# A graph network of two layers on one core: head outputs turned in 32x32 blocks by VectorE, and new aims for the planned order

## The chip, the cores and the metric

The kernel runs on one core of a Trainium2 chip. The core has TensorE (PE, matrix products into PSUM), VectorE (DVE), ScalarE (ACT), GpSimd (POOL) and SyncE (SP, which here only issues transfers), each with an instruction queue of its own. The metric is the device time in microseconds of one execution, the median of several runs.

## The reference, cut to what matters

There are 16 independent batches of N = 1024 nodes with 256 features. Layer 0 is attention with 8 heads of width 32; layer 1 is two graph attentions and a feed-forward part.

```python
# layer 0, for one batch
e = einsum('hqd,hkd->hqk', q, k)                 # q, k, v: 8 heads of 32 columns
e = where(e >= 0, e, 0.2 * e)
attn = softmax(where(adj > 0, e, NEG), axis=-1)
h = einsum('hqk,hkd->hqd', attn, v)              # head outputs
h = h.transpose to (n, 8 * 32)
out = layernorm(h, g1, b1)
out = concatenate([out, x], -1) @ Wffn.T
x1 = layernorm(out, g2, b2) + x
# layer 1: h = gat(gat(x1)); r = layernorm(x1 + h); layernorm(r + relu(r @ w_ff1) @ w_ff2)
```

The edit concerns the line of the head outputs and the division by the softmax's sums; the rest of the computation stays as it is.

## The kernel before, in words

All of a batch is computed with keys on the partitions. For head h and a tile t of 128 keys, `all_scores` (from L591) makes a score tile of 128 keys x 1024 queries in PSUM with two matmuls (L612). `weights` turns it into the tile `p`: ScalarE scales it by 0.2 (L628), VectorE takes the maximum with the scores (L630), ScalarE takes the exponential (L633), GpSimd multiplies by the mask of 0 and -1 (L637). Six `p` tiles exist at a time.

`all_values` multiplies the `p` tiles with V. One "product" is four matmuls side by side in four groups of 32 columns of the array: group i takes 256 queries of `p` and leaves 32 rows (the head's width) x 256 columns in partitions 32i to 32i+31 of `acc`, a PSUM bank. In the profile each of the four is recorded twice, as two passes over its 256 columns (L652). The left half of `acc` takes the product with V (stored negated), the right half the product with a tile of -1, which gives every partition of a group the same softmax sums. Two key tiles are taken at a time. For the first two pairs of a head VectorE first adds the two `p` tiles (L682, `add_pair`), so that six sums a head are made in place of eight.

`after_head` finishes a head. VectorE or ScalarE, whichever the planner finds free first, copies `acc` into an SBUF tile `ho` (L325 or L327 in `copy`); TensorE transposes `ho` in four 128x128 pieces into a PSUM bank `misc` (L702); VectorE takes the reciprocal of the sums (L707) and multiplies the outputs into `hn`, nodes on the partitions (L709). There are 128 heads in all. When a batch's eight heads are done, `rest` runs the remainder of the batch (transposes L369, products L778 and L781, the two graph attentions L863 to L926, feed-forward L966 and L994), beside the heads of the next batch.

The order on all five queues is fixed when the program is built. A planner (`Order`) keeps a clock for each engine, runs every part of the work as a thread whose steps state a cost (`yield on(PE=437)`), and puts next the ready step with the smallest "aim", a due time. Threads hold slots of counted buffers (three `misc` banks, one `acc`, six `p`, 18 `pair` tiles and others). The aims come from two tables, `EARLY` for the first two batches and `AIM` for the others, in units of a batch's slot of 253 us: `qk0` and `qk1` for the two halves of the next batch's Q and K projections, `v0` and `v1` for V, `graph0` and `graph1` for the graph attentions, `ff` for the feed-forward parts, `lead` for how early scores may start. `SWITCH` is the planner's cost of changing the shape in which TensorE is used ("single" for scores, "narrow" for products, None for the rest).

Transfers go out on two queues: x and the adjacency on ScalarE's, the projections' scratch writes, the stacks of Q and K that every head loads, x1 and the outputs on SyncE's.

Of the kernel before, what the change touches and what calls it, by code (L numbers as in the profile page):

```python
# [15 lines left out]
OP = mybir.AluOpType  # L16
# [18 lines left out]
class Order:  # L35
# [8 lines left out]
    SWITCH = {(None, "narrow"): 93.0, ("single", "narrow"): 93.0, ("narrow", None): 93.0,  # L44
              ("narrow", "single"): 197.0, (None, "single"): 84.0}
# [92 lines left out]
    def run(self):  # L138
        while self.active:
# [38 lines left out]
            if delay:  # L178
                self.transfers = max(self.transfers, end + 1000) + 1450 * max(1, round(cost / 500))
                th["ready"] = max(end + delay, self.transfers + 1200)  # L180
                th["last"] = None, 0
# [13 lines left out]
def wait(event):  # L195
    return "wait", event
# [37 lines left out]
def unshifted_path(  # L234
# [21 lines left out]
    ADDED = 2  # L256
# [144 lines left out]
    def mask_part(b, t, halves):  # L401
# [32 lines left out]
        yield on(PE=112 * n)  # L434
# [23 lines left out]
    def x_pair(b, u):  # L458
# [7 lines left out]
        yield on(PE=437)  # L466
# [47 lines left out]
    def v_part(b, g, u):  # L514
# [3 lines left out]
        yield on(PE=880)  # L518
# [72 lines left out]
    def all_scores():  # L591
        for b in range(B):
# [4 lines left out]
            for h in range(H):  # L597
                yield wait(("stack", b, h))
                q, kk = stacks[b, h]
                for t in range(NT):  # L600
# [8 lines left out]
                    yield on(PE=464, mode="single")  # L609
# [30 lines left out]
    def all_values():  # L640
        for b in range(B):
            for h in range(H):
# [7 lines left out]
                def product(w, p, at, first, last):  # L650
                    for i in range(4):
                        nc.tensor.matmul(acc[i * DH:(i + 1) * DH, at:at + QN], w, p[:, i * QN:(i + 1) * QN],  # L652
                                         start=first, stop=last)

                added = []
                for d in range(0, NT, GV):
                    last, adds = d + GV == NT, d < ADDED * GV
                    for t in range(d, d + GV):
                        yield wait(("p", b, h, t))
                    if added:  # L660
                        yield wait(("p added", b, h, d - GV))
                    yield aim(begin[b] + (h * NT + d + 2) / 2 * pace(b), SLOT)
                    ps = [probs.pop((b, h, t)) for t in range(d, d + GV)]
                    for t, p in zip(range(d, d + GV), ps):
                        yield on(PE=430, mode="narrow")
                        product(v[:, t, c:c + DH], p, 0, t == 0, False)
                        yield aim(begin[b], BIG)
                    if adds:
                        yield start(add_pair(b, h, d, ps), begin[b] + (h * NT + d + 2) / 2 * pace(b))
                    for p in added if adds else added + ps:  # L670
                        yield on(PE=430, mode="narrow")
                        product(minus_ones, p, QN, False, last and p is ps[-1])
                        yield give("p")
                    added = ps[:1] if adds else []
# [5 lines left out]
    def add_pair(b, h, d, ps):  # L680
        yield on(DVE=1180, shared=True)
        nc.vector.tensor_tensor(ps[0], ps[0], ps[1], op=OP.add)  # L682
        yield give("p")
        yield fire(("p added", b, h, d))

    def after_head(b, h, acc):
# [8 lines left out]
        engine = yield evacuate(HALF)  # L695
        copy(engine, ho, acc)
        yield give("acc")
        yield take("misc")
        pt = misc()
        yield on(PE=437)  # L700
        for i in range(TPH):
            nc.tensor.transpose(pt[:, i * P:(i + 1) * P], ho[:, i * P:(i + 1) * P], ident)  # L702
# [4 lines left out]
        nc.vector.reciprocal(rd, src[:, 1, :, :, 0])  # L707
        yield on(DVE=342)
        nc.vector.tensor_tensor(hn[b].rearrange("p (c i) d -> p i c d", i=2)[:, :, :, h * DH:(h + 1) * DH],  # L709
                                src[:, 0], rd[:, :, :, None].to_broadcast([P, 2, 4, DH]), op=OP.mult)  # L710
        yield give("misc")
# [39 lines left out]
    def rows_pair(b, u):  # L751
# [12 lines left out]
        yield on(PE=437)  # L764
# [26 lines left out]
        yield on(PE=437)  # L791
# [12 lines left out]
        for t in tiles:  # L804
            yield take("misc")
            pa = misc()
            yield on(PE=880)
# [28 lines left out]
    def first_half(b, s, nh):  # L836
# [7 lines left out]
        yield on(PE=437)  # L844
# [70 lines left out]
    def normed_pair(b, u, big, y2):  # L915
# [6 lines left out]
        for i, t in enumerate(tiles):  # L922
# [5 lines left out]
            yield on(PE=218)  # L928
# [10 lines left out]
        yield on(PE=437)  # L939
# [40 lines left out]
    def feed_forward(b, u, rT):  # L980
# [9 lines left out]
        for i in range(2):  # L990
# [5 lines left out]
            yield on(PE=218)  # L996
# [474 lines left out]
```

## Time and profile before

| | us |
|---|---|
| median of 3 runs (4397.36 to 4398.8) | 4397.64 |
| the profiled execution | 4397.53 |
| its span, first to last instruction | 4395.7 |
| TensorE matmuls busy | 4246.0 |
| VectorE busy | 3543.5 |
| ScalarE busy | 2979.7 |
| GpSimd busy | 2418.1 |

The span is that of the profiled execution; the 1.8 us beyond it lie before its first and after its last instruction. Busy time counts a matmul until its modelled end, so that overlapping matmuls count once. A line of the group list names the source line, the engine, the operation and its tiles, then the busy time in us and the mean ns of one instruction, and last the idle time just before these instructions with what ended it.

### The profile page before, as it was taken

Reading aid. Unit: us, or ns where it says so; the run is one execution under the profiler, and the core shown is the slowest. Engines: PE = TensorE matmul, PEld = TensorE weight load, DVE = VectorE, ACT = ScalarE, POOL = GpSimd, SP = SyncE. Lnnn points to the kernel's source line nnn. Section 1 sums busy time; section 2 is a strip of 40 time slices with the busy share of each in tenths; the row PEclk is TensorE's granted clock in tenths of the full one; section 3 lists DMA queues with packets and bytes.
Section 4 is the critical chain, followed back from the end, with each engine's and each line's share of the span. In section 5 each row is a group of like instructions: output and inputs, shape, how many; then the busy total and the mean of one; then the engine's idle time right before and its main releaser. Section 6 shows DMA issues by size and latency. Waiting matters only on the chain.

```text
span 4395.7 us, 77297 instructions
## 1 busy us (share of the span) xinstructions
PE 4246.0 (97%) x30539; PEld 3077.3 (70%) x30539; DVE 3543.5 (81%) x5525; ACT 2979.7 (68%) x4456; POOL 2418.1 (55%) x1033
## 2 busy tenths in 40 slices
PE   7888999999999999999999999999999999999898
PEld 4455767767677776767767677776767767677687
DVE  6878878878787888889788787888878788887853
ACT  6756667766767767776676767767776676766632
POOL 5856555554656646565564755636565564755700
PEclk9999999999999999999999999999999999999999
DMA  6423223232232323222232232313222232221100
GB/s 186 122 68 87 71 70 85 65 100 68 85 84 73 94 61 92 80 85 77 66 101 70 85 82 68 101 61 89 82 82 80 66 101 70 83 74 49 34 20 21
DMA packets 156287, 344.87 MB, mean 78 GB/s; under 512 B 21750, under 2 KB 24332, under 8 KB 155916
## 3 DMA queue, kind: packets, MB, share of 16 engines
q1 hardware_dynamic: 112140, 260.13, 20.5%
q10 hardware_dynamic: 43776, 79.71, 6.5%
q8 instruction: 243, 3.98, 0.4%
q14 instruction: 128, 1.05, 0.1%
HBM read 239.09 MB, written 100.66 MB: 77 GB/s over the span
## 4 chain that ended last, share of the span: by engine, by line
PE 81%; DVE 14%; ACT 3%; issue 2%; POOL 0%; DMA 0%; ACTq 0%; SPq 0%; DVEq 0%; POOLq 0%
PE ps_a L652 16%; PE ps_m L901 10%; PE ps_s L612 9%; PE ps_m L926 9%; PE ps_m L994 8%; PE ps_m L966 8%; DVE p L630 4%; PE ps_m L489 4%; PE ps_m L810 3%; DVE att L863 3%; PE ps_m L778 3%; PE ps_m L781 2%; DVE att L866 2%; PE ps_m L369 2%; PE ps_m L521 2%
## 5 line engine op out<-in xcount | busy, mean ns | idle before, releaser
L637 POOL TENSOR_TENSOR p<-p,mask 128x1024 f32<-128x1024 f32 x1024 | 2417.3, 2377 | 1752.1 <-ACT p L633 1401.4
L630 DVE TENSOR_TENSOR p<-p,ps_s 128x1024 f32<-128x1024 f32 x1024 | 1221.2, 1215 | 356.0 <-ACT p L628 351.5
L633 ACT ACTIVATE p<-p 128x1024 f32<-128x1024 f32 x1024 | 1080.2, 1060 | 343.3 <-DVE p L630 319.0
L628 ACT ACTIVATE p<-ps_s 128x1024 f32<-128x1024 f32 x1008 | 989.9, 1022 | 285.8 <-PE ps_s L612 202.5
L612 PE MATMUL ps_s<-qs,ks 128*128 128x512 f32 x2048 | 639.1, 430 | 35.5 <-DVE p L630 35.3
L652 PE MATMUL ps_a<-p,v 128*32 128x256 f32 x8192 | 564.1, 388 | 13.2 <-POOL p L637 12.6
L612 PEld LDWEIGHTS ps_s<-qs,ks 128*128 128x128 f32 x2048 | 350.0, 190 | 213.5 <-issue 68.0
L926 PE MATMUL ps_m<-y,att 128*128 128x256 f32 x2048 | 487.0, 382 | 5.8 <-ACT y L871 5.8
L901 PE MATMUL ps_m<-y,att 128*128 128x258 f32 x2048 | 482.8, 383 | 3.1 <-ACT y L871 2.6
L966 PE MATMUL ps_m<-rT,wf 128*128 128x256 f32 x2048 | 472.7, 381 | 13.2 <-ACT z L327 7.3
L994 PE MATMUL ps_m<-wf,hid 128*128 128x256 f32 x2048 | 475.3, 380 | 7.4 <-DVE hn L709 7.2
L901 PEld LDWEIGHTS ps_m<-y,att 128*128 128x128 f32 x2048 | 385.2, 190 | 85.6 <-issue 12.9
L966 PEld LDWEIGHTS ps_m<-rT,wf 128*128 128x128 f32 x2048 | 380.6, 190 | 81.8 <-issue 11.0
L652 PE MATMUL ps_a<-p,minus_ones 128*32 128x256 f32 x6144 | 408.7, 384 | 25.2 <-DVE p L682 25.2
L994 PEld LDWEIGHTS ps_m<-wf,hid 128*128 128x128 f32 x2048 | 379.9, 190 | 72.9 <-PE ps_a L652 12.2
L926 PEld LDWEIGHTS ps_m<-y,att 128*128 128x128 f32 x2048 | 376.7, 190 | 64.6 <-issue 8.6
L652 PEld LDWEIGHTS ps_a<-p,v 128*32 128x32 f32 x8192 | 209.0, 109 | 286.3 <-issue 143.3
L682 DVE TENSOR_TENSOR p<-p 128x1024 f32<-128x1024 f32 x256 | 385.4, 1506 | 25.7 <-PE ps_a L652 25.6
L863 DVE SCALAR_TENSOR_TENSOR att<-first,second 128x1024 f32<-128x1024 f32 x256 | 393.7, 1538 | 4.5 <-ACT first L850 4.5
L866 DVE SCALAR_TENSOR_TENSOR att<-mask,att 128x1024 f32<-128x1024 fp8e4 x256 | 353.0, 1379 | 5.9
L652 PEld LDWEIGHTS ps_a<-p,minus_ones 128*32 128x32 f32 x6144 | 198.7, 111 | 166.9 <-DVE p L682 32.1
L871 ACT ACTIVATE y<-y,check 128x258 f32<-128x258 f32 x256 | 130.8, 511 | 254.7 <-DVE check L869 254.2
(105 smaller groups left out, 4373.3 us busy)
## 6 DMA issues: line engine op xcount, KB each, us to landing
qs<-qk_halves SPq DMA_DIRECT2D x256, 256.0 KB, 4.1
ks<-qk_halves SPq DMA_DIRECT2D x256, 256.0 KB, 5.1
adj_i<-in_adj_dram ACTq DMA_DIRECT2D x240, 256.0 KB, 3.1
qk_halves<-high SPq DMA_DIRECT2D x128, 256.0 KB, 3.6
qk_halves<-low SPq DMA_DIRECT2D x128, 256.0 KB, 2.7
xr<-in_x_dram ACTq DMA_DIRECT2D x64, 256.0 KB, 2.7
x_kept<-x SPq DMA_DIRECT2D x64, 256.0 KB, 2.0
x<-x_kept SPq DMA_DIRECT2D x64, 256.0 KB, 3.4
```

The source lines that it names most:

```text
L612: nc.tensor.matmul(ps[:, cols], kk[:, t * P:(t + 1) * P], q[:, cols], start=True, stop=True)
L628: nc.scalar.activation(p, ps, AF.Copy, scale=ALPHA)
L630: nc.vector.tensor_tensor(p, p, ps, op=OP.max)
L633: nc.scalar.activation(p, p, AF.Exp)
L637: nc.gpsimd.tensor_tensor(p, p, mask_of(b, t), op=OP.mult)
L652: nc.tensor.matmul(acc[i * DH:(i + 1) * DH, at:at + QN], w, p[:, i * QN:(i + 1) * QN], start=first, stop=last)
L863: nc.vector.scalar_tensor_tensor(e, first[:, 0, :], second[:, j:j + 1], first[:, 1, :], op0=OP.mult, op1=OP.max)
L866: nc.vector.scalar_tensor_tensor(e, mask_of(b, j), -1.0, e, op0=OP.mult, op1=OP.mult, accum_out=sums[:, j:j + 1])
L901: nc.tensor.matmul(pa[:, cols:cols + width], big[:, j, i * P:(i + 1) * P], rows[:, j, :width], start=(j == 0), stop=(j == NT - 1))
L926: nc.tensor.matmul(pa[:, i * D:(i + 1) * D], big[:, j, t * P:(t + 1) * P], y2[:, j, :D], start=(j == 0), stop=False)
L966: nc.tensor.matmul(pa[:, i * 2 * P:(i + 1) * 2 * P], wf1[:, dc, hc * P:(hc + 1) * P], rT[:, dc, :], start=(dc == 0), stop=(dc == DC - 1))
L994: nc.tensor.matmul(pa[:, i * D:(i + 1) * D], hid[hc // 2][:, hc % 2, i * P:(i + 1) * P], wf2[:, hc, :], start=(hc == 0), stop=False)
```

## The change

Four things change.

The product takes its queries in another order: column group i takes, of each tile of 128 queries, the 32 with numbers 32i to 32i+31. The moving operand is then eight runs of 32 elements, 128 elements apart, and the output columns are ordered by tile and then by query in the run.

The head output is no longer copied and transposed by TensorE. VectorE's block transpose turns each 32x32 block of `acc` in place of the copy, PSUM to SBUF, and with the new order of queries the nodes then stand on the partitions as `hn` needs them. The reciprocal and the multiply read `ho` in SBUF.

The adding of `p` tiles is driven by tables (`JOINS`, `SUMMED`), which list the same two additions and six sums a head as before; a way of adding by a GpSimd transfer is written but not listed.

All values of `AIM` and `EARLY` are new, and so are `SWITCH` and several of the planner's costs, which touch the order of the instructions and nothing else.

```diff
-    SWITCH = {(None, "narrow"): 93.0, ("single", "narrow"): 93.0, ("narrow", None): 93.0,
-              ("narrow", "single"): 197.0, (None, "single"): 84.0}
+    SWITCH = {(None, "narrow"): 45.0, ("narrow", None): 250.0, ("narrow", "single"): 240.0}
...
-    ADDED = 2
+    JOINS = (('dve', 0, 1), ('dve', 2, 3))
+    SUMMED = ((0, 4), (2, 6), (4, 6), (5, 6), (6, 8), (7, 8))
+    JOINCOST = 950
+    JOINDELAY = 3600
...
-    AIM = dict(mask0=0.7454, x=0.7836, x_step=0.0012, mask=0.7416, mask_step=0.0241, qk0=0.8169, qk1=0.7629,
-               qk_step=0.0234, v0=0.8897, v1=0.9566, v_step=0.0513, rows=-0.1328, rows_step=0.039, first0=0.1101,
-               first1=0.2264, graph0=-0.041, graph1=0.3629, graph_step=0.0128, second=0.3518, second_step=0.0609,
-               normed=0.8572, normed_step=0.058, ff_wait=(None, 0, 1, 0), ff=(0.6792, -0.0021, 0.5781, 0.4984),
-               ff_step=0.0549, fast0=0.4291, fast1=0.9756, fast15=0.6646, lead=1.5024)
+    AIM = dict(mask0=0.5516, x=1.3927, x_step=-0.0171, mask=0.9041, mask_step=0.0013, qk0=0.7122, qk1=2.623,
+               qk_step=0.0074, v0=0.8646, v1=0.2387, v_step=-0.0163, rows=-0.0352, rows_step=0.0016, first0=0.4294,
+               first1=-0.1321, graph0=-0.0631, graph1=0.3632, graph_step=0.0462, second=0.6113, second_step=0.0151,
+               normed=1.0294, normed_step=0.0117, ff_wait=(None, 0, 1, 0), ff=(0.8041, 0.204, 3.2793, 1.5053),
+               ff_step=-0.1175, fast0=-0.0586, fast1=0.753, fast15=1.0361, lead=6.4585)
...
-    EARLY = dict(x=0.9697, x_step=0.0004, mask=0.7306, mask_step=0.0331, qk0=0.7893, qk1=0.9441, qk_step=0.026,
-                 v0=0.8496, v1=0.9733, v_step=0.0532, rows=-0.1833, rows_step=-0.0236, first0=0.1365,
-                 first1=-0.0311, graph0=-0.0903, graph1=-0.027, graph_step=0, second=0.3474, second_step=0.0327,
-                 normed=0.781, normed_step=0.02, ff_wait=(None, 0, 1, 0), ff=(0.6698, 0.0209, 0.488, 0.4266),
-                 ff_step=0.0422)
+    EARLY = dict(x=2.6793, x_step=-0.0501, mask=0.507, mask_step=0.0764, qk0=0.7919, qk1=0.9003, qk_step=-0.1061,
+                 v0=0.6048, v1=1.7324, v_step=-0.1383, rows=-2.2292, rows_step=-0.217, first0=-0.2174,
+                 first1=-4.0958, graph0=-0.094, graph1=-1.7727, graph_step=-0.0927, second=0.2445,
+                 second_step=0.079, normed=0.7931, normed_step=0.086, ff_wait=(None, 0, 1, 0),
+                 ff=(2.1852, 0.6139, 2.2145, 0.5745), ff_step=0.0569)
...
-        yield on(PE=437)
+        yield on(PE=460)
...
-        yield on(PE=880)
+        yield on(PE=895)
...
-                    yield on(PE=464, mode="single")
+                    yield on(PE=466, mode="single")
...
                 def product(w, p, at, first, last):
                     for i in range(4):
-                        nc.tensor.matmul(acc[i * DH:(i + 1) * DH, at:at + QN], w, p[:, i * QN:(i + 1) * QN],
+                        nc.tensor.matmul(acc[i * DH:(i + 1) * DH, at:at + QN].rearrange("d (t r) -> d t r", r=DH), w,
+                                         p.rearrange("k (t i r) -> k i t r", i=4, r=DH)[:, i],
                                          start=first, stop=last)
...
-                        yield on(PE=430, mode="narrow")
+                        yield on(PE=434, mode="narrow")
...
-    def add_pair(b, h, d, ps):
-        yield on(DVE=1180, shared=True)
-        nc.vector.tensor_tensor(ps[0], ps[0], ps[1], op=OP.add)
+    def join(b, h, n, ps):
+        how, to, by = JOINS[n]
+        for m in range(n):
+            if JOINS[m][1] in (to, by):
+                yield wait(("joined", b, h, m))
+        if how == "dve":
+            yield on(DVE=1180, shared=True)
+            nc.vector.tensor_tensor(ps[to], ps[to], ps[by], op=OP.add)
+        else:
+            yield on(POOL=JOINCOST, delay=JOINDELAY)
+            nc.gpsimd.dma_start(ps[to], ps[by], accum_op=OP.add)
         yield give("p")
-        yield fire(("p added", b, h, d))
+        yield fire(("joined", b, h, n))
...
         ho = buf([P, HALF], "pair", "ho")
-        engine = yield evacuate(HALF)
-        copy(engine, ho, acc)
+        yield on(DVE=600)
+        nc.vector.transpose(ho, acc)
         yield give("acc")
-        yield take("misc")
-        pt = misc()
-        yield on(PE=437)
-        for i in range(TPH):
-            nc.tensor.transpose(pt[:, i * P:(i + 1) * P], ho[:, i * P:(i + 1) * P], ident)
+        src = ho.rearrange("p (s t d) -> p s t d", s=2, d=DH)
+        rd = checks[b][:, h * NT:(h + 1) * NT]
+        yield on(DVE=205)
+        nc.vector.reciprocal(rd, src[:, 1, :, 0])
+        yield on(DVE=340, shared=True)
+        nc.vector.tensor_tensor(hn[b][:, :, h * DH:(h + 1) * DH], src[:, 0],
+                                rd[:, :, None].to_broadcast([P, NT, DH]), op=OP.mult)
         yield give("pair")
-        src = pt.rearrange("p (s i c d) -> p s i c d", s=2, i=2, d=DH)
-        rd = checks[b][:, h * NT:(h + 1) * NT].rearrange("p (c i) -> p i c", i=2)
-        yield on(DVE=235)
-        nc.vector.reciprocal(rd, src[:, 1, :, :, 0])
-        yield on(DVE=342)
-        nc.vector.tensor_tensor(hn[b].rearrange("p (c i) d -> p i c d", i=2)[:, :, :, h * DH:(h + 1) * DH],
-                                src[:, 0], rd[:, :, :, None].to_broadcast([P, 2, 4, DH]), op=OP.mult)
-        yield give("misc")
```

More of the change, by code (lines that the diff above doesn't have):

```diff
@@ L178, in run @@
             if delay:
-                self.transfers = max(self.transfers, end + 1000) + 1450 * max(1, round(cost / 500))
+                self.transfers = max(self.transfers, end + 1000) + (2700 if engine == "POOL" else
+                                                                    1450 * max(1, round(cost / 500)))
                 th["ready"] = max(end + delay, self.transfers + 1200)
@@ L433, in mask_part @@
         pairs = ab.bitcast(BF)
-        yield on(PE=112 * n)
+        yield on(PE=30 + 140 * n)
         for i in range(2 * n):
@@ L651, in product @@
                     for i in range(4):
-                        nc.tensor.matmul(acc[i * DH:(i + 1) * DH, at:at + QN], w, p[:, i * QN:(i + 1) * QN],
+                        nc.tensor.matmul(acc[i * DH:(i + 1) * DH, at:at + QN].rearrange("d (t r) -> d t r", r=DH), w,
+                                         p.rearrange("k (t i r) -> k i t r", i=4, r=DH)[:, i],
                                          start=first, stop=last)
-                added = []
+                ps = {}
+                begun = 0
@@ L656, in all_values @@
                 for d in range(0, NT, GV):
-                    last, adds = d + GV == NT, d < ADDED * GV
+                    last = d + GV == NT
                     for t in range(d, d + GV):
                         yield wait(("p", b, h, t))
[L660 to L664, printed above, removed]
-                        yield on(PE=430, mode="narrow")
-                        product(v[:, t, c:c + DH], p, 0, t == 0, False)
-                        yield aim(begin[b], BIG)
@@ L668, in all_values @@
[L668 to L672, printed above, removed]
+                    now = [t for t, at in SUMMED if at == d + GV]
+                    for t in now:
+                        for n in range(begun):
+                            if JOINS[n][1] == t:
+                                yield wait(("joined", b, h, n))
@@ new lines, in all_values @@
+                    due = begin[b] + (h * NT + d + 2) / 2 * pace(b)
+                    yield aim(due, SLOT)
+                    for t in range(d, d + GV):
+                        ps[t] = probs.pop((b, h, t))
+                        yield on(PE=434, mode="narrow")
+                        product(v[:, t, c:c + DH], ps[t], 0, t == 0, False)
+                        yield aim(begin[b], BIG)
+                    while begun < len(JOINS) and max(JOINS[begun][1:]) < d + GV:
+                        yield start(join(b, h, begun, ps), due)
+                        begun += 1
@@ L673, in all_values @@
+                    for t in now:
+                        for n in range(begun):
+                            if JOINS[n][1] == t:
+                                yield wait(("joined", b, h, n))
+                        yield on(PE=434, mode="narrow")
+                        product(minus_ones, ps[t], QN, False, last and t == now[-1])
                         yield give("p")
-                    added = ps[:1] if adds else []
                 yield start(after_head(b, h, acc), begin[b] + (h + 1) * NT // 2 * pace(b))
@@ L763, in rows_pair @@
         pt = misc()
-        yield on(PE=437)
+        yield on(PE=460)
         transposes(pt, rows)
@@ L790, in rows_pair @@
         pt = misc()
-        yield on(PE=437)
+        yield on(PE=460)
         transposes(pt, rows)
@@ L806, in rows_pair @@
             pa = misc()
-            yield on(PE=880)
+            yield on(PE=895)
             w = YW + 2
@@ L843, in first_half @@
         pt = misc()
-        yield on(PE=437)
+        yield on(PE=460)
         for i in range(TPH):
@@ L927, in normed_pair @@
                                      start=(j == 0), stop=False)
-            yield on(PE=218)
+            yield on(PE=225)
             as_rows(pa, i, x1, i)
@@ L938, in normed_pair @@
         pt = misc()
-        yield on(PE=437)
+        yield on(PE=460)
         transposes(pt, rows)
@@ L995, in feed_forward @@
                                      start=(hc == 0), stop=False)
-            yield on(PE=218)
+            yield on(PE=225)
             as_rows(pa, i, rT, i)
```

## The prediction

> **What bounds the kernel now.** I read the engine totals first, then the stretches, then TensorE's own order of work, then the rows that the edit touches. Totals:
>
> ```profile
> PE 4246.0 (97%) x30539; PEld 3077.3 (70%) x30539; DVE 3543.5 (81%) x5525; ACT 2979.7 (68%) x4456; POOL 2418.1 (55%) x1033
> ```
>
> TensorE is busy 97% of the span. That average hides stages, so here are stretches cut at repeats of the same instruction in the chain of work (columns: from:to, length, busy time and count of each engine, granted clock, DMA share, GB/s):
>
> ```profile
> 0.00:440.00 440.00, 366.16 (x2751) 222.52 (x2752) 340.54 (x435) 294.77 (x397) 282.16 (x127) 0.93 0.40 116
> 440.00:1184.02 744.02, 724.16 (x5264) 519.72 (x5263) 603.46 (x948) 518.85 (x770) 421.30 (x181) 1.00 0.27 78
> 1184.02:1448.35 264.33, 261.65 (x1906) 191.37 (x1905) 219.82 (x346) 186.34 (x279) 150.33 (x65) 1.00 0.28 81
> 1448.35:1712.70 264.35, 261.62 (x1906) 191.34 (x1905) 219.83 (x345) 186.35 (x279) 150.35 (x65) 1.00 0.28 80
> 3829.30:4176.00 346.70, 330.90 (x2468) 240.73 (x2467) 296.43 (x444) 232.37 (x334) 211.93 (x87) 0.99 0.19 53
> 4176.00:4395.70 219.70, 207.55 (x1018) 180.43 (x1016) 102.81 (x261) 69.62 (x176) 0.00 (x0) 0.98 0.06 20
> ```
>
> In the middle of the run each batch takes 264.3 us, and TensorE is busy for 261.6 of them with full clock: there the time is TensorE's instruction stream and nothing else. VectorE, the next engine, has 219.8. Only the ends differ: the first 440 us leave TensorE idle for 73.8 us at a clock of 0.93, 440 to 1184 for 19.9, 3829 to 4176 for 15.8 and the tail for 12.2. Work taken from TensorE's stream should therefore shorten the middle one for one.
>
> **1. The four transposes go.** TensorE's timeline (start, length, instruction, how many):
>
> ```profile
> 2003.02 1.89 PE L926 MATMUL ps_m<-y,att 128*128 128x256 f32 x8
> 2004.84 1.07 PE L652 MATMUL ps_a<-p,v 128*32 128x256 f32 x16
> 2005.73 0.61 PE L652 MATMUL ps_a<-p,minus_ones 128*32 128x256 f32 x8
> 2006.28 1.99 PE L926 MATMUL ps_m<-y,att 128*128 128x256 f32 x8
> ...
> 2021.69 1.17 PE L612 MATMUL ps_s<-qs,ks 128*128 128x512 f32 x4
> 2022.70 0.60 PE L702 MATMUL ps_m<-ident,ho 128*128 128x128 f32 x4
> 2023.14 1.89 PE L926 MATMUL ps_m<-y,att 128*128 128x256 f32 x8
> 2024.87 0.38 PE L436 MATMUL ps_m<-ident_b,adj_b 128*128 128x128 bf16 x4
> ```
>
> The group's shown length is 0.60 us, but the next matmul starts 0.44 us after its first one (2022.70 to 2023.14). What the stream gets back is 0.44, since the rest is pipelined latency: 128 heads x 0.44 = **56.3 us**, or 3.5 us of each 264.3 us batch. Here a rule and a row differ. The Trainium skill, "TensorE: Matmul & The Clock Gate", Part 4 on PE-mode transposes, gives about 275 ns for a transpose inside a kernel. That is the duration of one in this trace too, but 512 x 275 ns would promise 141 us. The start-to-start spacing decides: 56.3. The group's busy time, 78.3 us below, is an upper end.
>
> **2. What else the rows of a head show** (group list: count, busy us, mean ns, idle before):
>
> ```profile
> L702 PE MATMUL ps_m<-ident,ho 128*128 128x128 f32 x512 | 78.3, 275 | 4.0 <-ACT mask L440 2.5 <-DVE rT L386 0.4 <-ACT columns L327 0.3
> L325 DVE COPY ho<-ps_a 128x512 f32<-128x512 f32 x74 | 51.0, 690 | 26.6 <-PE ps_a L652 26.4
> L327 ACT COPY ho<-ps_a 128x512 f32<-128x512 f32 x54 | 31.4, 582 | 29.8 <-PE ps_a L652 29.7
> L707 DVE RECIPROCAL check<-ps_m 128x8 f32<-128x8 f32 x128 | 26.2, 205 | 50.3 <-PE ps_m L702 50.0
> L994 PE MATMUL ps_m<-wf,hid 128*128 128x256 f32 x2048 | 475.3, 380 | 7.4 <-DVE hn L709 7.2 <-DVE hid L972 0.2
> ```
>
> TensorE also stands 4.0 us before the transposes and 7.2 us before L994 for a "misc" bank that L709 still reads. Both waits lose their cause, as the head output no longer takes such a bank; but an order with a gap closed may meet the next one (a fraction of a us later in each batch). Ends 0 and 11.2; I take the middle, **-6 us**.
>
> **3. VectorE's side.** The copy to ho was VectorE's for 74 heads and ScalarE's for 54; now all 128 are VectorE block transposes. No such instruction is in the trace. The nearest row is the copy of the same shape, 0.690 us, and I take that. The upper end is a page's: the skill's "VectorE: DVE Perf Modes", the section on three transpose paths, has 311 ns for 128 columns, so four times that, 1.24 us, for 512 (an estimate from that page). By the row, VectorE gains 54 x 0.69 = 37 us of work; by the page 128 x 1.24 - 51 = 108 us. Per batch that is +2.3 or +6.8.
>
> The multiply into hn changes its source from PSUM to SBUF, and one rule speaks against that. The skill's "SBUF — State Buffer", "SBUF: two separate sides", says that a VectorE instruction with two SBUF inputs and a GpSimd instruction lock each other out for a whole instruction. The durations (least/median/greatest ns) agree:
>
> ```profile
> L709 DVE TENSOR_TENSOR hn<-ps_m,check x128: 424/424/427, 65.7 to 4176.2; 128x256 f32<-128x256 f32 x128
> L1005 DVE SCALAR_TENSOR_TENSOR z<-z,mv,gl x128: 452/478/2270, 497.6 to 4388.1; 128x256 f32<-128x256 f32 x128
> ```
>
> With PSUM as source the multiply never took over 427 ns; z, with SBUF sources and the same width, reaches 2270 and has a mean of 560. By the row before, nothing would be added; by the row with the lock, 128 x (560 - 424) = 17 us, or 1.1 us a batch, which I take. GpSimd is kept out for under half a us each time, against the 114 us per batch in which it is not busy. VectorE then has 219.8 + 2.3 + 1.1 = 223.2 us per batch (227.7 by the page) against TensorE's new 258: it stays cover. It also loses a stall: 50.0 us of VectorE idleness before the reciprocal, waiting for L702 with everything in its queue behind it (the p maxima that the scores wait for). In its place all 128 transposes wait in that queue for the last product, 26.4 us / 74 x 128 = 46 us by today's copies; so VectorE's stalls are a draw. ScalarE loses 31 us, off the path. **0 us** on the end. If the cover were gone, the 37 + 17 us would count in full.
>
> **4. The products read p in runs of 32.** Same 14,336 matmuls, same 256 columns, but eight runs of 128 bytes a row instead of one of 1,024; the output stays contiguous. No row shows a moving operand in runs. The nearest is L652 itself, contiguous: three products (two passes each) between 2004.84 and 2006.28, 0.48 us each with the switch of array shape in it. I take **0**. The other end is priced by the columns: a 256-column pass takes 216 ns (eight between 2023.14 and 2024.87), 0.84 ns a column; one column lost at each of 8 x 7,168 run starts would be +48 us. The planner's cost for a product goes from 430 to 434 ns; taken at its word that is 3,584 x 4 ns = 14 us, but in the same edit unchanged instructions are raised too (464 to 466, 880 to 895).
>
> **5. Joins.** The new tables list the sums that the old loop made: the pairs (0,1) and (2,3) added on VectorE, six sums a head at the same places, with the same waits. The GpSimd branch of join is not entered. **0**.
>
> **6. The new order.** The aims and the planner's costs change the static order of all five queues. In the middle it can give nearly nothing: 2.7 us idle per batch. It can give at the ends, where idleness beyond the middle's 1% is 69 + 12 + 12 + 10, about 104 us; it can also lose there or open new holes in the middle. Gain half, loss of the same size: between -50 and +100. Nothing in the profile says which, so **0**.
>
> Sum: 4397.5 us of the profiled execution (span 4395.7 and 1.8 around it, 0.1 under the median of the runs) - 56.3 - 6 = **4335 us**, 0.986 of before. Its own range, from parts 1 to 5 (-78 to +14, and some 20 either way for the order), is 4310 to 4365.
>
> **Rivals.**
>
> *The ends fill too* (4290): the new start values close two thirds of the 69 us in the first 440 us, 45 us more. For: there TensorE waits 21.9 us for L630 and 19.3 for L682, VectorE work that order can move forward. Against: the chain of work begins there with two transfers of 6.4 and 4.8 us, which no order shortens.
>
> *A hole in each batch* (4439, slower): "qk1" becomes 2.62 slots in the later batches, so that the second half of the next batch's Q and K projections ranks behind nearly all else, while head 4 wants their stacks 1.5 slots after the batch's due time begins. They run only when TensorE has nothing better, and from there the chain is one matmul group (1.7 us), ScalarE 0.6, VectorE 0.7, a write on SP's queue of about 3.6 us, and four stack loads behind it of about 5 us: 12 us before the first score of head 4. If other work covers a third, 8 us x 13 batches = 104 us. It decides from 62 / 13 = 4.8 us a batch. Against: feed-forward work of TensorE is put later still (3.3 and 1.5 slots) and could fill the hole.
>
> *Run starts cost columns* (4383 with one column at each, 4431 with two; 48 us apiece): break-even is at 1.3 columns. Against: a run is 128 bytes long.
>
> *VectorE becomes the bound*: at 223 to 228 of 261 us it needs another 30 us a batch of waits in its queue; then about 4400, no change.
>
> **How the numbers follow.** Chances: my forecast 0.60, ends fill 0.17, hole 0.13, run starts 0.07 (half of it still faster), VectorE 0.03. A measurement can tell 0.2% (9 us) from no change. Faster 0.60 + 0.17 + 0.035 = 0.80; slower 0.13 + 0.03 = 0.16; the same 0.04. The range is 4280 to 4415: above lies most of the hole case and the two-column case, below a complete closing of the ends, together under 2 in 10.
>
> **What would show it.** Right: TensorE's count falls by 512, the batch period in the middle falls from 264.3 to about 260.8, L652's mean stays at 384 to 388 ns, VectorE has 128 transposes near 0.69 us and a multiply mean near 560. Wrong: longer spacing inside L652; a repeated TensorE wait at L612 for stacks or for L630; a first stretch longer than 440 us to the same instruction.

## The result and the profile after

The changed kernel takes **4319.5 us** (median of 4 runs, 4314.6 to 4324.1) against 4398.2 for the kernel before in the same series: a ratio of 0.9821, with a 95% interval of 0.9804 to 0.9838. It is 78.7 us faster. The prediction had 4335, with an own range of 4310 to 4365. The total was met to 16 us, but by luck: two terms that had been set at nothing were large and nearly cancelled.

The profiled execution of the changed kernel took 4324.1 us, its span is 4322.2. Its engine totals, on the page:

```profile
PE 4182.5 (97%) x30027; PEld 3040.8 (70%) x30027; DVE 3662.3 (85%) x5631; ACT 2940.4 (68%) x4350; POOL 2469.1 (57%) x1033
```

TensorE has 512 matmuls and 63.5 us of busy time less. VectorE has 119 us more (3543.5 before), where the prediction had counted 37 + 17. The stretches of the changed kernel, with the columns of the prediction's:

```profile
0.00:440.00 440.00, 359.00 (x2624) 214.60 (x2625) 324.53 (x431) 281.79 (x378) 267.13 (x123) 0.90 0.38 112
440.00:1193.63 753.63, 737.41 (x5364) 531.49 (x5363) 656.09 (x982) 541.71 (x796) 461.42 (x191) 1.00 0.29 80
1452.51:1711.42 258.91, 257.09 (x1874) 188.97 (x1873) 229.85 (x354) 183.05 (x269) 154.31 (x64) 1.00 0.29 82
4102.00:4322.20 220.20, 206.90 (x1005) 177.52 (x1004) 102.33 (x260) 67.94 (x172) 0.00 (x0) 0.99 0.06 21
```

A batch in the middle now takes 258.9 us, 5.4 less than before, where 3.5 were expected. The start is no better: TensorE idles 81 us in the first 440 (73.8 before), at a granted clock of 0.90 (0.93 before). Most of the gain is in the middle, and a part of it is seen in TensorE's timeline of the changed kernel:

```profile
2377.92 1.07 PE L655 MATMUL ps_a<-p,v 128*32 128x256 f32 x16
2378.81 1.48 PE L655 MATMUL ps_a<-p,minus_ones 128*32 128x256 f32 x24
2380.11 1.05 PE L655 MATMUL ps_a<-p,v 128*32 128x256 f32 x16
2380.97 1.05 PE L655 MATMUL ps_a<-p,minus_ones 128*32 128x256 f32 x16
2381.95 1.99 PE L980 MATMUL ps_m<-rT,wf 128*128 128x256 f32 x8
```

Two pairs of key tiles, nine products, follow each other without leaving the narrow shape. Counted over TensorE's whole order, the kernel before enters that shape 547 times and the changed one 493; in a batch of the middle 35 times and 29. One visit costs 0.33 us in the trace of before, by the medians: the first product starts 309 ns after the last wide pass (216 is usual), its second pass comes 24 ns late, the next wide instruction starts 309 ns after the last narrow pass (196 is usual), and its second pass of 256 columns comes 320 ns after its first (216 is usual). Six visits fewer are 2.0 us a batch, about the 1.9 us that the transposes do not explain.

VectorE's adding of p before the change, and then its rows of the changed kernel at the end of a head, with the adding of p (L699):

```profile
L682 DVE TENSOR_TENSOR p<-p 128x1024 f32<-128x1024 f32 x256 | 385.4, 1506 | 25.7 <-PE ps_a L652 25.6
```

```profile
L699 DVE TENSOR_TENSOR p<-p 128x1024 f32<-128x1024 f32 x256 | 439.4, 1716 | 26.4 <-PE ps_a L655 26.3
L723 DVE TENSOR_TENSOR hn<-ho,check 128x256 f32<-128x256 f32 x128 | 104.1, 813 | 2.3
L716 DVE STREAM_TRANSPOSE ho<-ps_a 128x512 f32<-128x512 f32 x128 | 91.3, 713 | 28.2 <-PE ps_a L655 28.0
L721 DVE RECIPROCAL check<-ho 128x8 f32<-128x8 f32 x128 | 25.9, 203 | 4.1
```

The transpose is near the copy's 690 ns. The multiply is not at the 560 ns that was taken but at 813, and the adding of p, which had 1506 ns, takes 1716, 54 us more in all. The next sections ask what that costs and why the time fell all the same.

### The profile page after: what moved, and what is told of

It reads as the page before. It is cut to its first block, busy times and chain, and to the rows that moved or that the text cites. A ratio compares the mean times of both kernels' runs of the same rounds, so it can differ in the third digit from the quotient of the medians.

```text
span 4322.2 us, 76295 instructions
## 1 busy us (share of the span) xinstructions
PE 4182.5 (97%) x30027; PEld 3040.8 (70%) x30027; DVE 3662.3 (85%) x5631; ACT 2940.4 (68%) x4350; POOL 2469.1 (57%) x1033
## 4 chain that ended last, share of the span: by engine, by line
PE 78%; DVE 13%; ACT 5%; issue 2%; POOL 1%; DMA 1%; ACTq 0%; SPq 0%; POOLq 0%; DVEq 0%
PE ps_a L655 16%; PE ps_m L915 10%; PE ps_s L615 10%; PE ps_m L1008 9%; PE ps_m L940 9%; PE ps_m L980 8%; DVE p L633 5%; PE ps_m L492 4%; PE ps_m L792 3%; PE ps_m L824 3%; PE ps_m L795 2%; ACT p L631 2%; PE ps_m L372 2%; PE ps_m L524 2%; DVE p L699 2%
## 5 line engine op out<-in xcount | busy, mean ns | idle before, releaser
L640 POOL TENSOR_TENSOR p<-p,mask 128x1024 f32<-128x1024 f32 x1024 | 2468.3, 2429 | 1629.5 <-ACT p L636 1161.9
L633 DVE TENSOR_TENSOR p<-p,ps_s 128x1024 f32<-128x1024 f32 x1024 | 1213.3, 1212 | 219.6 <-ACT p L631 217.1
L615 PE MATMUL ps_s<-qs,ks 128*128 128x512 f32 x2048 | 662.2, 439 | 39.2 <-DVE p L633 36.2
L655 PE MATMUL ps_a<-p,v 128*32 128x256 f32 x8192 | 561.7, 390 | 12.0 <-POOL p L640 11.4
L615 PEld LDWEIGHTS ps_s<-qs,ks 128*128 128x128 f32 x2048 | 354.1, 190 | 258.1 <-issue 112.8
L1008 PE MATMUL ps_m<-wf,hid 128*128 128x256 f32 x2048 | 476.6, 381 | 12.7 <-DVE xT L328 6.3
L699 DVE TENSOR_TENSOR p<-p 128x1024 f32<-128x1024 f32 x256 | 439.4, 1716 | 26.4 <-PE ps_a L655 26.3
L1008 PEld LDWEIGHTS ps_m<-wf,hid 128*128 128x128 f32 x2048 | 379.1, 190 | 75.3 <-ACT hid L989 9.0
L655 PE MATMUL ps_a<-p,minus_ones 128*32 128x256 f32 x6144 | 408.3, 383 | 3.9 <-DVE p L699 3.9
L655 PEld LDWEIGHTS ps_a<-p,v 128*32 128x32 f32 x8192 | 216.4, 110 | 265.1 <-issue 133.0
L880 DVE SCALAR_TENSOR_TENSOR att<-mask,att 128x1024 f32<-128x1024 fp8e4 x256 | 365.6, 1428 | 6.0
L877 DVE SCALAR_TENSOR_TENSOR att<-first,second 128x1024 f32<-128x1024 f32 x256 | 346.4, 1353 | 9.3 <-ACT first L864 8.9
L655 PEld LDWEIGHTS ps_a<-p,minus_ones 128*32 128x32 f32 x6144 | 199.2, 111 | 144.3 <-issue 10.7
```

Of the source, the lines that this page charges most:

```text
L615: nc.tensor.matmul(ps[:, cols], kk[:, t * P:(t + 1) * P], q[:, cols], start=True, stop=True)
L633: nc.vector.tensor_tensor(p, p, ps, op=OP.max)
L640: nc.gpsimd.tensor_tensor(p, p, mask_of(b, t), op=OP.mult)
L655: nc.tensor.matmul(acc[i * DH:(i + 1) * DH, at:at + QN].rearrange("d (t r) -> d t r", r=DH), w, p.rearrange("k (t i r) -> k i t r", i=4, r ...
L699: nc.vector.tensor_tensor(ps[to], ps[to], ps[by], op=OP.add)
L880: nc.vector.scalar_tensor_tensor(e, mask_of(b, j), -1.0, e, op0=OP.mult, op1=OP.mult, accum_out=sums[:, j:j + 1])
```

## The experiments

The theory at the start was the prediction's, with one thing added after the result: the stream of TensorE is the time, VectorE lies beside it, and the order gives some 16 us by fewer entries. The rivals: the new order carries the gain and the new head would lose without it; the runs of 32 cost something that another gain hides.

Since the kernel before was run beside each series and drifts a little (4398 to 4403), differences are taken against it within the series.

| kernel | median | difference to before | ratio, 95% interval |
|---|---|---|---|
| changed kernel | 4319.5 | -78.7 | 0.9804 to 0.9838 |
| new head, old aims and costs | 4463.0 | +61.0 | 1.0127 to 1.0158 |
| old head, new aims and costs | 4503.5 | +101.5 | 1.0217 to 1.0248 |
| changed, whole runs | 4323.6 | -78.4 | 0.9804 to 0.9831 |
| changed, four more transposes, early | 4462.9 | +60.9 | 1.0124 to 1.0155 |
| changed, four more transposes, in place | 4374.3 | -25.2 | 0.9922 to 0.9955 |
| changed, transpose costed 680 | 4474.9 | +75.4 | 1.0149 to 1.0183 |
| changed, turned twice | 4452.2 | +52.7 | 1.0103 to 1.0136 |
| old order kept, new head | 4438.1 | +38.6 | 1.0065 to 1.0099 |
| old order kept, new head, no lock | 4379.1 | -20.5 | 0.9936 to 0.9969 |
| the same, 54 heads unturned | 4366.9 | -34.6 | 0.9907 to 0.9941 |
| changed, no lock | 4309.1 | -94.1 | 0.9784 to 0.9811 |

"No lock" is short for a multiply with one of its inputs in PSUM; the section on the old order says why. The intervals are some 0.15% wide either way, so a difference between two rows is uncertain by about 10 us.

Five of the six kernels that are slower than before also ran at a lower granted clock: 0.980 to 0.987 in the mean of the profiled execution, against 0.990 before. As an estimate, 0.001 of the clock is at most 4.4 us, so that 13 to 44 us of their time may lie there. Whether their waits lowered the clock was not tested.

### The two parts apart: the head, and the aims

The first mix is the kernel before with the new `product` and the new `after_head`; the second is the changed kernel with the old ones.

```diff
 # new head, old aims: before.py with
-        engine = yield evacuate(HALF)
-        copy(engine, ho, acc)
+        yield on(DVE=600)
+        nc.vector.transpose(ho, acc)
 # ... and the rest of after_head and product as in the change; AIM, EARLY, SWITCH and costs as before
```

> The kernel before with the new product and the new end of a head alone; aims, switch costs and the planner's other costs as before. If the four transposes are the main term and the order the rest, the time is 4397.6 - 56 - 0 to 6: 4336 to 4342, a batch in the middle takes 264.3 - 3.5 = 260.8 us, and TensorE still enters the narrow shape about 547 times. If the gain is the new order's and the removed transposes are replaced by a wait, it is over 4370. If the new order is needed for VectorE's heavier load, it is over 4350 with waits of TensorE for VectorE's p that the changed kernel does not have.

> The changed kernel with the old product and the old end of a head (copy, four transposes, multiply from PSUM); aims, switch costs and the other planner costs are the new ones. If the order is worth the 15 to 20 us that the transposes do not explain, and is so whatever the head does: 4375 to 4385, with fewer than 520 entries into the narrow shape. If the new order is worth nothing without the new head: 4395 to 4405 and about 545 entries. If it was fitted to the new head so closely that it loses without it: over 4410.

Both are slower than either kernel, by 61 and 101.5 us over the one before. No value that was expected of the first theory holds; those of the rivals do (over 4370 for the first, over 4410 for the second). In both, the batches of the middle have no common length any more: from the end of one batch's last product to the next, 261 to 275 us in the first mix and 265 to 274 in the second, where the kernel before repeats 264.3 and the changed one 258.9. That the aims had been chosen for other durations, so that the order no longer falls into a repeat, is likely but not shown by these two.

So these two mixes do not separate head and order: each has a new order of its own. The later ones, but for one, therefore keep an order fixed.

### Does reading p in runs cost anything?

```diff
-                        nc.tensor.matmul(acc[i * DH:(i + 1) * DH, at:at + QN].rearrange("d (t r) -> d t r", r=DH), w,
-                                         p.rearrange("k (t i r) -> k i t r", i=4, r=DH)[:, i],
+                        nc.tensor.matmul(acc[i * DH:(i + 1) * DH, at:at + QN], w, p[:, i * QN:(i + 1) * QN],
```

> The changed kernel with the old reading of p in the product (256 queries in one run), everything else and the order as in the changed kernel; the head outputs then stand at other queries' places, so what is left out is the right order of the nodes. If runs of 32 cost TensorE nothing: within 4 us of the changed kernel (4315 to 4324), and the spacing inside L655 stays 0.216 us a pass. If they cost 4 ns a product, as the planner's number has it: 14 us less, about 4305. If they cost a column per run start: 48 us less, about 4272.

-78.4 us against the changed kernel's -78.7: no difference. The rows of the product in the changed kernel, and then with whole runs:

```profile
L655 PE MATMUL ps_a<-p,v 128*32 128x256 f32 x8192 | 561.7, 390 | 12.0 <-POOL p L640 11.4
L655 PE MATMUL ps_a<-p,minus_ones 128*32 128x256 f32 x6144 | 408.3, 383 | 3.9 <-DVE p L699 3.9
```

```profile
L655 PE MATMUL ps_a<-p,v 128*32 128x256 f32 x8192 | 562.3, 391 | 13.4 <-POOL p L640 12.8
L655 PE MATMUL ps_a<-p,minus_ones 128*32 128x256 f32 x6144 | 407.9, 383 | 3.2 <-DVE p L698 3.2
```

Means and busy times are the same, and so is the median spacing of two passes, 216 ns in both. The planner's 434 in place of 430 ns is not a cost of the runs.

### What four transposes a head cost in TensorE's stream

The order of the changed kernel was kept and four transposes of a constant were put in, first where the head's bank is taken, then directly before the head's first product (this second form is the one printed).

```diff
...
+                        if t == 0:
+                            for i in range(TPH):
+                                nc.tensor.transpose(acc[:, i * P:(i + 1) * P], ident, ident)
                         product(v[:, t, c:c + DH], ps[t], 0, t == 0, False)
```

> The changed kernel with four transposes of a constant into the head's own bank just before its first product, unknown to the planner, so that the order of all else is that of the changed kernel. If TensorE's stream is what a batch lasts: 128 x 0.44 = 56 us more, 4376, and up to 128 x 0.23 = 29 us on top where they part two products that now follow each other in the narrow shape, so 4376 to 4405. If TensorE has slack that hides them: under 4345.

> The changed kernel with four transposes of a constant put directly before a head's first product, where the bank is free anyway; the order of all else is kept. The first try stood earlier and cost 143 us, of which TensorE waited 86.1 for the bank. If the price of the transposes is their place in TensorE's stream: 56 us more, about 4376, and up to 29 more where they part two visits of the narrow shape, so 4376 to 4405. If the first try's 143 us were a real price: over 4440.

The early place costs 139.6 us (from -78.7 to +60.9), more than either expectation. TensorE's waits say why: the transposes stood in its queue ahead of other work and waited for the bank.

```profile
PE ps_a L653 <- DVE ho L718: 86.1, 99, 4.0
```

TensorE's idle time grew by 73 us in all (139.6 to 212.9) and its busy time by 60. In place they cost 53.5 us (from -78.7 to -25.2), which is 0.42 us a head, as expected: TensorE's busy time grows by 57 us (4182.5 to 4239.4) and its idle time by 2. In the trace they set the first product back by 0.44 us (it starts 745 ns after the last wide pass in place of 309). The step of 56.3 us for the transposes is right within the 10 us that this difference is uncertain. A batch of the middle goes from 258.9 to 263.2, 0.53 us a head; why it is more there was not followed.

### Is VectorE cover?

```diff
         nc.vector.transpose(ho, acc)
+        nc.vector.transpose(ho, acc)
```

> The changed kernel with each block transpose done twice, unknown to the planner: 128 x 0.71 = 91 us more on VectorE, order kept. If VectorE lies wholly beside TensorE, as the prediction has it: at most 10 us more, under 4330. If its queue is nearly the bound: 40 us or more, over 4360; with no cover at all, 4410.

It costs 131.5 us: the 4452.2 are far over the 4360 of "nearly the bound" and over the 4410 of "no cover at all". That is more than the 91.8 us of the added transposes. But VectorE's busy time grew by 185 us (3662.3 to 3847.2), twice what was added, as other rows became longer too. The engine totals with two transposes, and the multiply, which took 813 ns with one:

```profile
PE 4221.4 (95%) x30027; PEld 3034.3 (68%) x30027; DVE 3847.2 (86%) x5759; ACT 2936.5 (66%) x4350; POOL 2455.1 (55%) x1033
L724 DVE TENSOR_TENSOR hn<-ho,check 128x256 f32<-128x256 f32 x128 | 170.8, 1334 | 2.3
```

So the run does not price 91.8 us of VectorE's work alone: it moved the multiply to places where it waits longer, which added 67 us. Set against all 185 us, each microsecond of VectorE cost 0.7 of the kernel's time. VectorE is busy 85% of the span, and yet it is only a partial cover. TensorE's waits with one transpose (the changed kernel), and then with two (waited for, us in total, times, longest):

```profile
PE ps_s L615 <- DVE p L633: 36.2, 43, 3.5
PE ps_a L655 <- POOL p L640: 11.4, 11, 2.7
```

```profile
PE ps_s L615 <- DVE p L633: 69.1, 97, 3.8
PE ps_a L655 <- POOL p L640: 29.4, 46, 2.9
PE ps_m L861 <- DVE v L531: 19.9, 11, 1.8
```

The maxima of p (L633) come later, since VectorE takes its queue in order. They free the score banks, so TensorE waits for a bank (L615), and they are links of the chain to the masked p, so TensorE waits for p (L655). These visible waits are 71 of the 89 us by which TensorE's idle time grew (139.6 to 228.4). Its busy time grew by 39 us for the same matmuls as well (4182.5 to 4221.4). A matmul's record (some 390 ns) is longer than the spacing to the next (216), so a wait shorter than that lies inside the busy time; that this is where the rest went was not shown otherwise.

### The new head with the old order kept

Here the planner is left with all its old steps and costs, and only what is emitted changes, so that the instructions common to both kernels stand in the same order on all five queues.

```diff
         engine = yield evacuate(HALF)
-        copy(engine, ho, acc)
+        nc.vector.transpose(ho, acc)
         yield give("acc")
         yield take("misc")
-        pt = misc()
         yield on(PE=437)
-        for i in range(TPH):
-            nc.tensor.transpose(pt[:, i * P:(i + 1) * P], ho[:, i * P:(i + 1) * P], ident)
... (product, reciprocal and multiply read as in the change)
```

> The kernel before with every queue in its old order, and only the head's end exchanged: VectorE's block transpose stands where the copy stood, the four transposes are left out, the product reads runs of 32. The planner still counts the old costs, so nothing else moves. If the sum of the prediction holds by itself, without a new order: 4397.6 - 56 - 0 to 6 = 4336 to 4342, and a batch in the middle takes 260.8 us. If the removed transposes only uncover another wait: 4370 to 4395. If the heavier VectorE needs another order, as the slow mix of old aims and new head suggests: over 4400.

4438.1, 38.6 us slower than before: the third case. The sum of parts 1 to 5 of the prediction, by itself, was not a gain of 62 us but a loss. By the ends of the batches the whole loss lies in the first five (41 us); the ten in the middle take as long as before (264.1 us against 264.3), so that there VectorE eats what the transposes give. The row of VectorE that stands out, with its least, median and greatest duration below:

```profile
L709 DVE TENSOR_TENSOR hn<-ho,check 128x256 f32<-128x256 f32 x128 | 162.9, 1273 | 4.4
L709 DVE TENSOR_TENSOR hn<-ho,check x128: 424/1354/2403, 65.2 to 4222.5; 128x256 f32<-128x256 f32 x128
```

In place of 425 ns the multiply takes 1273, which is 109 us of VectorE's time. Of the 128, 76 took over 570 ns; all of these began while a GpSimd instruction ran and ended 277 to 289 ns after it; those that began with GpSimd idle took at most 427 ns. The next kernel removes the multiply's second SBUF input: the reciprocals go to the PSUM bank that the planner still reserves there, and a small copy by ScalarE takes them on to SBUF.

```diff
+        pt = misc()
...
-        nc.vector.reciprocal(rd, src[:, 1, :, 0])
+        nc.vector.reciprocal(pt[:, :NT], src[:, 1, :, 0])
...
-                                rd[:, :, None].to_broadcast([P, NT, DH]), op=OP.mult)
+                                pt[:, :NT, None].to_broadcast([P, NT, DH]), op=OP.mult)
+        nc.scalar.copy(rd, pt[:, :NT])
```

> The new head in the old order of all queues once more, but the reciprocals go into the PSUM bank that the planner still reserves there, so that the multiply has one input in SBUF and one in PSUM; ScalarE copies the reciprocals (128 small copies) to where they are counted. In the run before this the multiply took 1273 ns a time in place of 425, 109 us in all, and the time was 4438. If VectorE's wait for GpSimd in that multiply is what ate the gain: the multiply falls to about 425 ns and the time to 4340 to 4370. If it is the copies that ScalarE no longer shares (54 x 0.69 = 37 us more on VectorE) and their wait for TensorE: 4415 to 4440, no change.

```profile
L709 DVE TENSOR_TENSOR hn<-ho,ps_m x128: 420/421/424, 65.1 to 4158.2; 128x256 f32<-128x256 f32 x128
```

The multiply is back at 421 ns, never more than 424, though 79 of the 128 began beside a GpSimd instruction. VectorE's busy time falls by 151 us (3719.9 to 3569.1), since the adding of p and others become shorter too. The time falls by 59.1 us to 20.5 under the kernel before. The size lies between the two expectations; that VectorE's wait for GpSimd, called the lock here, is the cause is shown. Of the profiled executions' 64 us, 37 lie in the first five batches. A batch of the middle goes from 264.1 to 262.2 us and TensorE's stretches (old order with the lock, and without) differ in idle time, 5.0 us against 3.4:

```profile
2372.30:2636.40 264.10, 259.08 (x1880) 187.58 (x1872) 228.66 (x349) 184.95 (x276) 149.78 (x64) 1.00 0.29 81
```

```profile
2325.50:2587.70 262.20, 258.81 (x1880) 187.83 (x1872) 220.03 (x349) 185.88 (x284) 149.56 (x64) 1.00 0.29 81
```

There are still 33 us missing to the 53.5 of the transposes. One more kernel, like the last, takes away the rest of VectorE's new work: the 54 heads that ScalarE had copied are copied by it again.

```diff
-        nc.vector.transpose(ho, acc)
+        nc.vector.transpose(ho, acc) if engine == "DVE" else nc.scalar.copy(ho, acc)
```

A first form, in which the multiply took the unturned outputs, has no time: its quotients left the range of a later logarithm. In the form that ran, the multiply of these heads takes the sums in place of the outputs, which are left out.

> The new head in the old order, without the lock (4379), and now ScalarE copies the 54 heads that it copied before the change; these heads are not turned at all and their outputs are left out (the multiply runs on the sums in their place and gives ones). VectorE then has no work more than before the change, and TensorE lacks the four transposes. If the 33 us by which the lock-free version misses the 56 us are VectorE's extra 37 us: 4340 to 4350. If they are something else (the small ScalarE copies of the reciprocals, or waits that the removed transposes uncover): 4365 to 4380.

34.6 us under the kernel before: 14 us of the 33 were VectorE's extra 37 us (its busy time falls by 30), and the time lies in the range of the second expectation. Of the other 19, the small ScalarE copies that only these experiments have account for a part. TensorE waits for them in this kernel:

```profile
PE ps_m L996 <- ACT check L712: 10.1, 12, 0.9
PE ps_m L848 <- ACT check L712: 5.0, 10, 0.5
```

These are 15.1 us. But the kernel before waits 7.2 us in the first of the two places, for a bank of the same kind, so the copies' own share is nearer 8 us (an estimate from these waits); the other 11 were not found. The kernel with the lock has no such waits, so the lock's price in the old order may be up to 15 us above the 59.

### The same instructions in another order

```diff
-        yield on(DVE=600)
+        yield on(DVE=680)
         nc.vector.transpose(ho, acc)
```

> The changed kernel with one number of the planner changed: the block transpose is costed 680 ns in place of 600 (it takes 713). Every instruction is the same and only the order differs. If the order is a small matter, worth 10 to 20 us: 4310 to 4340. If the aims fit one set of costs and no other: over 4400, with batches of unequal length in place of 258.9 us each.

With this one planner's cost nearer to the measured 713 ns, the time is 154 us over the changed kernel's (from -78.7 to +75.4). The batches take 255 to 279 us, without a repeat, and TensorE enters the narrow shape 511 times. A truer cost, with the aims left as they were, made a worse order.

### The new order without the lock

In the changed kernel's order the transposes of 120 heads can be written back into the head's own bank, so that the multiply reads PSUM and SBUF.

```diff
+        if (b, h) not in SOON:      # eight heads of the first four batches, whose bank is needed sooner
+            ho = acc
         nc.vector.transpose(ho, acc)
... (one bank, acc, is made once and kept for all heads)
```

> The changed kernel in its own order, with the block transpose written back into the PSUM bank of the head (in place) for 120 of the 128 heads, so that the multiply reads PSUM and SBUF and not SBUF twice. For eight heads of the first four batches, where the next head's products are put before the multiply, ho stays in SBUF. VectorE loses up to 50 us of waiting in the multiply (104.1 us busy, 54.3 before the change). If the new order still pays for that lock at the rate of the old one (59 us of time for 109 us of VectorE): 4285 to 4300. If the new order already hides it, since TensorE is busy 257.0 of each 258.9 us: 4310 to 4322. If holding the bank until the multiply is done makes TensorE wait for it at a head's start: over 4330.

4309.1 us, 94.1 under the kernel before and 15.3 under the changed one by the differences of their series, with nothing left out. Beside the uncertainty of 10 us that is a small gain over the changed kernel. It lies between the first two expectations. The multiply, and the transpose in place:

```profile
L721 DVE STREAM_TRANSPOSE ps_a<-ps_a 128x512 f32<-128x512 f32 x120 | 87.4, 728 | 27.8 <-PE ps_a L658 27.5
L728 DVE TENSOR_TENSOR hn<-ps_a,check 128x256 f32<-128x256 f32 x120 | 50.6, 421 | 2.3
```

A batch of the middle goes from 258.9 to 258.3, and 7 of the profiled executions' 15 us come from the first batch (223.9 to 217.1). Those 7 us may be the clock's: the first 215 us of the changed kernel, and then of this one, were granted 0.88 and 0.92.

```profile
0.00:215.00 215.00, 170.57 (x1217) 85.08 (x1217) 150.23 (x160) 141.15 (x178) 146.01 (x71) 0.88 0.49 143
0.00:215.00 215.00, 169.82 (x1285) 86.06 (x1285) 147.16 (x166) 145.40 (x184) 151.15 (x73) 0.92 0.53 153
```

The lock costs some 15 us in the new order, against 59 or more in the old one, mainly since it takes less of VectorE there: its busy time falls by 46 us without it (3662.3 to 3615.8), by 151 in the old order. The price of one microsecond of VectorE is 0.3 and 0.4, not clearly different.

## Why the prediction was right, and where it was not

**The balance.** Against the kernel before: the four transposes 53.5 us less (measured in the new order, and taken over to the old one); the rest of the new head in the old order 92 us more, which makes the +38.6; the new order for that same head 117 us less (from +38.6 to -78.7). The sum is the -78.7. The prediction had -56.3, -6, and twice nothing. So the total was met by luck: nothing in the prediction ties the 92 to the 117. Its own range does not follow from its parts either: -78 to +14 on 4397.5 is 4319 to 4412, before the 20 either way for the order.

**Part 1, the transposes: right.** 56.3 against 53.5. Taking the spacing and not the duration or the busy time was the right reading; TensorE's busy time fell by 63.5 in all, with fewer entries in it.

**Part 2, the waits of 4.0 and 7.2 us: not a gain.** The 7.2 us before L994 went, and 6.3 and 5.9 us before the same line (now L1008) came in their place, for other releasers. The end at 0 was the right one.

**Part 3, VectorE "0 us on the end": wrong.** The transpose itself was sized well, 713 ns against 690 taken. Two steps failed. The multiply's wait for GpSimd was sized by z's row, 560 ns; it was 1273 in the old order (109 us of VectorE in place of 17) and 813 in the new, and the adding of p, not counted at all, took 42 and 54 us more. The rule on the shared lock was the right one to raise, but its price hangs on where GpSimd's instruction of 2.4 us stands, and the row of another instruction doesn't tell that. And the cover was read off busy shares: 223 of 258 us seemed to leave 35 us a batch. With a kept order VectorE's time was never free, and never paid in full: 151 us less paid 59 us or somewhat more, 30 us less paid 14, 46 us less paid 15, and 185 us more cost 131. So neither the "0 us" nor "the 37 + 17 us would count in full" describes it; between 0.3 and 0.7 of VectorE's time counted.

**Part 4, the runs: right**, 0 us, shown by the exchange. But its other ends were too large by two. The 14,336 records of L652 are passes, and four run side by side: 3,584 passes one after the other, two to each of 1,792 products. A planner's cost of 4 ns more a product is then 7 us, not 14, and one column lost at each run start 24 us, not 48. The measured difference of 0.3 us, uncertain by 10, speaks against the 24; against the 7 stands the spacing, which would be 218 ns and is 216.

**Part 5, the joins:** nothing in the traces speaks against 0; it was not tried by itself.

**Part 6, the order "0", and "in the middle it can give nearly nothing": wrong.** Only TensorE's idle time was counted as what an order could give, 2.7 us a batch. But the busy time holds visits to the narrow shape (six fewer a batch, 2.0 us), and an order can also keep or lose what VectorE's new work takes: for the new head, the new order is worth 117 us over the old one. Of these, by the ends of the batches, 57 are won up to the fifth batch, 54 in the ten batches of the middle and 7 in the last heads.

**The rivals.** The start did not fill; the run starts cost nothing. The hole by `qk1` did not come: in the changed kernel's first stretch and after, TensorE waits for the stacks once, 1.8 us. "VectorE becomes the bound" was given 3 in 100 and in its pure form did not happen. In the old order it was half right: at a busy share of 84%, VectorE's added work ate the whole gain.

Of the new order's 117 us, 78 are TensorE's visible idle time (217.8 to 139.6) and 39 its busy time (4221.9 to 4182.5). Fewer visits to the narrow shape are about 18 of these 39 (an estimate, 54 x 0.33). What stays open is the rest of the busy time, short waits or clock, and which of the new aims made the difference.

## What to carry to other kernels

A second engine at 83% that works its queue in order in the middle of a chain is only a partial cover: here 0.3 to 0.7 us of time went with each microsecond of its work. One way to test it is a run in which its new instruction is done twice, but then its whole busy time must be compared, since here it grew by twice what was added. A kernel whose order is written out by a planner should be tested with the order kept fixed, and again with the order fitted anew: here the two answers were +38.6 and -78.7 us. Two SBUF inputs on VectorE beside a busy GpSimd are worth a look each time: leaving one of them in PSUM brought 59 us in the one order and some 15 in the other.

## What the runs showed of the hardware that was not expected

- The multiply of 128x256 took at most 427 ns with one input in PSUM, in the kernel before and in the kernels without the lock, beside GpSimd's work or not. With both inputs in SBUF its least time was 405, its mean 813 in the changed kernel and 1273 in the old order, and its greatest 2403; the long ones ended 0.28 us after the GpSimd instruction beside which they began.
- VectorE's block transpose of 128x512 float32 elements takes 713 ns from PSUM to SBUF, where the plain copy takes 690, and 728 in place in PSUM.
- TensorE reads a moving operand in runs of 128 bytes, 512 bytes apart, as fast as in one run: 216 ns a pass of 256 columns both ways.
- A visit to the narrow shape cost TensorE 0.33 us, of which a third (104 ns) shows only at the second pass after it.
